# Order of the logarithm and the taps in a state-space mixer, and residual loads ahead of an inverse transform

## The chip, the core and the metric

The kernel runs on one core of one Trainium2 chip. A core has a matrix engine (TensorE, PE in the profile, with its weight loads as PEld), a vector engine (VectorE, DVE), an activation engine (ScalarE, ACT), a general engine (GpSimd, POOL) and SyncE (SP), whose only work here is to issue DMAs. Sixteen DMA engines move data between DRAM and the on-chip memory SBUF; matmuls write to PSUM. Everything is float32. The metric is the device time of one execution in microseconds: before the change 1432.75 us, the median of three runs (1431.81 to 1436.02).

## The reference, cut to what matters

The input is x of 8 images, 1024 tokens each, 128 channels. Three layers follow each other, each added to a residual:

```python
x = x + _L0_conv_ref(_gn(x), ...)               # attention, 4 heads of 32
t = _to_tokens(x)
t = t + _L1_attn_ref(_ln_t(t), ...)             # state-space mixer, both directions
t = t + _L1_ffn_ref(_ln_t(t), ...)              # spectral filters
```

The mixer computes, for each direction, a projection of the normalised tokens into a gate z, a part x, B, C and step sizes dt. x, B and C pass through a causal convolution of four taps and Silu; dt is a softplus:

```python
conv = sum((xp[:, i:i + l, :] * conv_w[:, i] for i in range(K))) + conv_b
xbc = jax.nn.silu(conv)
dt = jax.nn.softplus(dt + dt_bias)
```

The states of 64-token chunks are then built, carried from chunk to chunk with a decay, and read by C; the result is multiplied by silu(z), normalised and projected to 128 channels. The second direction does the same on the tokens in reverse.

The last layer filters the sequence with 16 spectral filters and their alternating-sign versions, by multiplication in the frequency domain, mixes channels with matrices for each filter, and adds a short autoregressive part.

## The kernel before, in words

**Attention.** The first 460 us or so. A loop over 128 steps (8 images, two halves of the queries, 8 blocks of keys) whose order is written out by hand; the step numbers n decide what of the next stages is slipped in. At steps 113 to 123 the first image's tokens are turned and its step sizes computed by the generator `steps` (L482), whose `yield`s cut it into pieces: matmuls for dt (L495), bias and negative absolute value on DVE (L504 to L507), Exp on ACT (L509), 1 + e on DVE and Ln on ACT (L512, L514), and the rest on DVE (L516 to L521).

**Mixer.** About 460 to 1000 us. There are 16 units, one for each image b and direction d (0 forward, 1 backward), in the order (0,0), (0,1), (1,0) and so on. The order on every engine, SP included, is the order of the program text (`manual_schedule(engines=ALL_IN_ORDER)`), so an instruction that waits holds back everything behind it on its engine. In the body of the loop over units, `u` is the unit whose states are built, `following` the one whose inputs are prepared, and `last` the one whose outputs are finished. In a forward unit `fresh` is the next image, whose tokens are turned and whose step sizes are computed piece by piece with `next(going)`. This is so in the units 0, 2, 4, 6, 8, 10 and 12.

The steps that the change and the prediction touch, in their order within a unit: `project_x` and `copy_x` of `following` (L935, L955); `end(last)` with its output projection (`spo`, L1166), sums of squares and reciprocal root; `first_tap(following, 0)` on ACT (L960); `scale_rows(last)` on ACT (L1204); the piece of `steps` with Ln; two of the three other taps of block 0 of `following` on DVE (`convolve`, L968); the two gates of `u`, each a projection on PE (`pz`, L935) and a Silu on ACT (L981); `first_tap(following, 1)`; `from_row` on POOL, a difference of cumulated decays (L912), which carries a written dependency on the last DVE operation of `convolve` so that it runs beside the states; a Relu pair on ACT (L922); `chunk_states` on PE (`pst`, L1070) and `pass_states` on DVE (a copy L1084, then 28 products L1087); the last piece of `steps`; the remaining tap of block 0, its Silu (L973), `project_bc` on PE (`pb`, L990), `activate_bc` on ACT (L1006), and the taps of block 1. PSUM tiles of projections, `pb` and the transposes share one pool of two buffers (`ps_w`), so `pb` waits until the first gate has been read. The states use another pool (`ps_s`).

An activation function belongs to a table set. The compiled program loads a set (`ACT_TABLE_LOAD`) where the next function needs another one than the current: Exp before Ln is one change, Ln before Silu another.

**Filters.** From about 1000 us the tokens are transformed; from 1116 us a loop over 16 chunks of 8 frequencies makes matrices on PE (`matrices`, L1500, from a tile `mst`), copies them to a tile `gs` (two buffers; L1511 and L1513), multiplies the spectra `u` with them (`apply`, L1534), and stores the sums to DRAM (`yd`, L1557). For the first of four output pieces, `fetch` (L1565) brings back each chunk's sums into `early_yt`. In this stage the scheduler keeps the program's order on PE, DVE, ACT and POOL, and places the DMA issues of SP itself.

**Tail.** Four pieces (k, h): two halves of the token blocks by two halves of the images. For each, `yt` (2 MB, two DMAs, L1600) and `res` (1 MB of the residual stream `xa`, L1602) are loaded; DVE forms four sums and differences `z` (L1608); PE makes four products of 128 x 512 over two terms (L1613); DVE multiplies by `keep`, adds the residual in place (L1620), and ACT's queue stores 1 MB (L1623). The pieces' pools are opened after those of the filter stage: two buffers for `yt`, three for `res`, four PSUM buffers.

Of the kernel before, what the change touches and what calls it, by code (L numbers as in the profile page):

```python
# [14 lines left out]
P = 128  # L15
# [30 lines left out]
def fast_kernel(ctx: ExitStack, tc: tile.TileContext, a: dict, out: bass.AP, bad: bass.AP):  # L46
# [433 lines left out]
    def steps(b, seq, pd):  # L480
# [31 lines left out]
        nc.vector.tensor_scalar(u, e, 1.0, None, ALU.add)  # L512
        lg = small("sp_l")
# [77 lines left out]
    with ExitStack() as s:  # L591
# [182 lines left out]
        for n in range(len(units) + 2):  # L774
# [33 lines left out]
            elif n == 113:  # L808
                turn_tokens(0, seqs[0], ps_t.tile([P, T], F32, tag="t", name="px0"))
            elif n == 117:  # L810
                sizes = steps(0, seqs[0], ps_t.tile([P, T], F32, tag="t", name="pd0"))
                for _ in range(3):
                    next(sizes)
            elif n in (121, 123):
                next(sizes, None)
# [10 lines left out]
    with ExitStack() as s:  # L826
# [438 lines left out]
        for at, u in enumerate(units[:-1]):  # L1265
# [46 lines left out]
            convolve(following, 0, range(pad - 1))  # L1312
# [3 lines left out]
            first_tap(following, 1)  # L1316
            for _ in normalized(b, bridge, *norm) if u.d else ():
                pass
# [8 lines left out]
            convolve(following, 0, range(pad - 1, pad))  # L1327
# [86 lines left out]
    with ExitStack() as s:  # L1414
        mp = s.enter_context(tc.tile_pool(name="c_m", bufs=1, side="right"))
        mst = mp.tile([P, 32, C], F32, name="mst")
# [68 lines left out]
        with ExitStack() as s2:  # L1485
# [80 lines left out]

            chunks = NF // FC
            gs, us, gathered = {}, {}, {}
            s2.enter_context(tc.manual_schedule(engines=IN_ORDER))
            for c in range(-1, chunks):  # L1570
                if c + 1 < chunks:
                    gs[c + 1] = p2.tile([P, P, C], F32, tag="gs", name=f"gs{c + 1}")
                    us[c + 1] = loaded_spectra(c + 1)

# [14 lines left out]
        with ExitStack() as s2:  # L1589
            p2 = s2.enter_context(tc.tile_pool(name="i_2", bufs=2))  # L1590
            p3 = s2.enter_context(tc.tile_pool(name="i_3", bufs=3))
            ps_o = s2.enter_context(tc.tile_pool(name="i_ps_o", bufs=4, space=PSUM))

            def loaded(k, h):

                yt = early_yt
                if k or h:
                    yt = p2.tile([P, 2, 4, 4, C], F32, tag="yt", name=f"yt{k}_{h}")
                    for i in range(2):
                        nc.sync.dma_start(yt[:, i], yd[:, k, h * 4 : h * 4 + 4, i])  # L1600
                res = p3.tile([P, 4, 4, C], F32, tag="res", name=f"res{k}_{h}")
                nc.sync.dma_start(res, xa[h * 4 : h * 4 + 4, :, NB - 1 - k].rearrange("b p r c -> p b (r c)"))  # L1602
                return yt, res

            def back(k, h, yt, res):
                z = p2.tile([P, 2, 2, 4, C], F32, tag="z", name=f"z{k}_{h}")
# [3 lines left out]
                for r in (0, 2, 1, 3):  # L1610
                    po = ps_o.tile([P, 4, C], F32, tag="o", name=f"pz{k}_{h}_{r}")
                    for i in range(2):
                        nc.tensor.matmul(  # L1613
                            po,
                            lhsT=inv[:, r, i, :],
                            rhs=z[:, r // 2, i] if r % 2 else yt[:, i, :, r // 2, :],
                            start=(i == 0),
                            stop=(i == 1),
                        )
                    nc.vector.scalar_tensor_tensor(  # L1620
                        res[:, :, r, :], po, keep[:, blk : blk + 1], res[:, :, r, :], ALU.mult, ALU.add
                    )
                nc.scalar.dma_start(  # L1623
                    out[h * 4 : h * 4 + 4, blk * 512 : (blk + 1) * 512].rearrange("b (p r) c -> p b (r c)", r=4), res
                )

            pieces = [(k, h) for k in range(NB) for h in range(2)]
            got = [loaded(*piece) for piece in pieces[:3]]
            for n, piece in enumerate(pieces):
                back(*piece, *got[n])  # L1630
                if n + 3 < len(pieces):
                    got.append(loaded(*pieces[n + 3]))
# [806 lines left out]
```

## Time and profile before

| | us |
|---|---|
| median of three runs | 1432.75 |
| the profiled execution | 1432.01 |
| its span, first to last instruction | 1430.2 |
| PE busy | 1334.7 (93%) |
| DVE busy | 1095.4 (77%) |
| ACT busy | 914.5 (64%) |
| POOL busy | 529.5 (37%) |
| last product of the filter stage ends | 1380.1 |
| last addition of a residual ends | 1423.2 |

Lines of the timeline give the start in us from the span's beginning, the busy time, engine, line of the source, operation, what it writes and reads (`out<-in`), and in brackets the engine's idle time before it with what ended that. Lines of the list of waits give who waited, for whom, the sum in us, how often, and the longest. A line of the table by slices gives the slice, its length, busy time and instructions of PE, PEld, DVE, ACT and POOL, the granted clock of PE (1.00 is full), the mean busy share of the DMA engines, and the GB/s that they moved. SPq and ACTq are DMA issues. A float32 matmul appears as two records.

### The profile page before, as it was taken

To read this page: it belongs to the slowest core of one execution; us is meant where nothing else is said; L and a number is where in the kernel's file an instruction comes from. 1 tells how busy PE (TensorE), PEld (TensorE's weight loads), DVE (VectorE), ACT (ScalarE), POOL (GpSimd) and SP (SyncE) were. 2 spreads that over 40 slices of the span, in tenths; PEclk is the share of its full clock that TensorE was granted. 3 is DMA by queue.
4 is the path that set the end of the run, shared out by engine and by line. 5 is a ranking of instruction groups with operands and counts; after the bars stand their busy time and mean duration, and the time that the engine had idled before them with its cause. 6 is when DMAs were issued, how large, how long until landed. Compare 5 with 4: busy or idle time off the path is not lost. (4 is left out here: it accounts for less than half of the span.)

```text
span 1430.2 us, 45285 instructions
## 1 busy us (share of the span) xinstructions
PE 1334.7 (93%) x19782; PEld 839.8 (59%) x19782; DVE 1095.4 (77%) x2138; ACT 914.5 (64%) x1421; POOL 529.5 (37%) x510
## 2 busy tenths in 40 slices
PE   5999999999998899999999999998799899999977
PEld 2323333233333566666666666666689899999963
DVE  5779888788768588979787988889644677777745
ACT  3665666766757678778787878786454555555520
POOL 3327866875610243324242424233476111111100
PEclk9999999999999899999999999999999999999989
DMA  7100111110000433434343444442459232222258
GB/s 182 40 1 21 55 38 38 38 51 25 8 1 19 102 76 79 100 90 105 75 105 88 94 92 114 95 106 46 132 190 232 73 89 76 71 77 70 72 153 324
DMA packets 139382, 123.09 MB, mean 86 GB/s; under 512 B 44808, under 2 KB 118152, under 8 KB 135080
## 3 DMA queue, kind: packets, MB, share of 16 engines
q1 hardware_dynamic: 137064, 115.93, 31.6%
q8 instruction: 157, 2.57, 0.8%
q10 hardware_dynamic: 2112, 4.19, 0.8%
q14 instruction: 49, 0.40, 0.1%
HBM read 78.15 MB, written 34.08 MB: 78 GB/s over the span
## 5 line engine op out<-in xcount | busy, mean ns | idle before, releaser
L696 ACT ACTIVATE pr<-pt 128x1024 f32<-128x1024 f32 x256 | 248.1, 1021 | 115.1 <-PE pt L691 113.5
L721 DVE TENSOR_TENSOR two<-pr,pr 128x1024 f32<-128x1024 f32 x128 | 162.9, 1313 | 20.5 <-ACT pr L696 19.6
L1513 ACT COPY gs<-pg 128x512 f32<-128x512 f32 x256 | 132.6, 602 | 64.4 <-PE pg L1500 47.9
L1511 DVE COPY gs<-pg 128x512 f32<-128x512 f32 x256 | 158.7, 682 | 15.3 <-PE pg L1500 9.6
L691 PE MATMUL pt<-q,k 32*128 32x512 f32 x1024 | 159.8, 654 | 7.0 <-ACT pr L696 4.7
L1500 PE MATMUL pg<-taps,mst 32*128 32x128 f32 x4096 | 146.0, 281 | 4.9 <-ACT gs L1513 4.1
L1500 PEld LDWEIGHTS pg<-taps,mst 32*128 32x128 f32 x4096 | 134.0, 189 | 17.1 <-issue 11.6
L712 PE MATMUL po<-pr,v 128*32 128x512 f32 x1024 | 139.9, 605 | 0.0
L926 POOL TENSOR_TENSOR ec<-ec,ct 128x2048 f32<-128x2048 f32 x16 | 83.4, 5212 | 135.3 <-ACT cums L868 59.2
L990 PE MATMUL pb<-bxt,wbc 128*128 128x512 f32 x256 | 116.9, 610 | 13.9 <-ACT zs L981 11.3
L1534 PE MATMUL py<-gs,u 128*32 128x128 f32 (+1 forms) x4096 | 127.8, 277 | 0.0
L968 DVE SCALAR_TENSOR_TENSOR xs<-xp,cw,xs 128x1024 f32<-128x1024 f32 x96 | 121.8, 1281 | 3.5 <-issue 1.7
L1534 PEld LDWEIGHTS py<-gs,u 128*32 128x32 f32 (+1 forms) x4096 | 112.0, 140 | 7.2
L1523 POOL TENSOR_SCALAR u<-u 128x512 f32<-128x512 f32 x16 | 24.0, 1498 | 229.3 <-PE pg L1500 128.5
L691 PEld LDWEIGHTS pt<-q,k 32*128 32x128 f32 x1024 | 47.6, 186 | 85.0 <-issue 32.2
L990 PEld LDWEIGHTS pb<-bxt,wbc 128*128 128x128 f32 x256 | 48.2, 193 | 73.1 <-issue 55.6
L1087 DVE SCALAR_TENSOR_TENSOR state<-state,dec,pst 128x64 f32<-128x64 f32 x448 | 87.3, 274 | 1.1
L1196 POOL TENSOR_TENSOR rms<-rms_v,mhalf 128x8 f32<-128x8 f32 x16 | 27.2, 1698 | 161.2 <-DVE rms_v L1194 161.2
L712 PEld LDWEIGHTS po<-pr,v 128*32 128x32 f32 x1024 | 27.8, 109 | 88.5 <-issue 84.6
L912 POOL TENSOR_TENSOR lm<-cs,lm 128x2048 f32<-128x2048 f32 x16 | 57.9, 3621 | 50.2 <-DVE xs L968 33.8
L732 PE MATMUL pd<-two,ones 128*32 128x512 f32 x512 | 73.0, 613 | 0.2
L1166 PEld LDWEIGHTS spo<-wo,y 128*128 128x128 f32 x512 | 62.1, 191 | 15.3 <-issue 10.3
(280 smaller groups left out, 2763.8 us busy)
## 6 DMA issues: line engine op xcount, KB each, us to landing
lm<-cd SPq DMA_DIRECT2D x32, 512.0 KB
ec<-cd SPq DMA_DIRECT2D x32, 512.0 KB
ud<-sp SPq DMA_DIRECT2D x8, 1024.0 KB
u<-ud SPq DMA_DIRECT2D x32, 256.0 KB
yd<-sums SPq DMA_DIRECT2D x32, 256.0 KB
moved<-state SPq DMA_DIRECT2D x48, 128.0 KB
yt<-yd SPq DMA_DIRECT2D x6, 1024.0 KB
X<-in_x SPq DMA_DIRECT2D x8, 512.0 KB
```

The lines of the kernel that those rows point to most:

```text
L691: nc.tensor.matmul(pt[:, i, :], lhsT=k[rows, j * P : (j + 1) * P], rhs=q[rows, cols], start=True, stop=True)
L696: nc.scalar.activation(pr[:, 2 * g : 2 * g + 2, :].rearrange("p i t -> p (i t)"), pt.rearrange("p i t -> p (i t)"), AF.Exp, scale=SCALE,)
L712: nc.tensor.matmul(po[rows, :], lhsT=vs[b][:, j, rows], rhs=pr[:, h, :], start=(j == 0), stop=(j == NT - 1))
L721: nc.vector.tensor_tensor(two, sums["pr"][:, 2 * g : 2 * g + 2, :], pr[:, 2 * g : 2 * g + 2, :], ALU.add)
L926: t = nc.gpsimd.tensor_tensor(u.ec, u.ec, u.ct.unsqueeze(1).to_broadcast([P, NH, NT, L]), ALU.mult)
L968: u.convolved = nc.vector.scalar_tensor_tensor(acc, xp[:, at : at + T], cw[u.d][:, n, i : i + 1], acc, ALU.mult, ALU.add)
L990: nc.tensor.matmul(u.pb[:, i * 512 : (i + 1) * 512], lhsT=wbc[u.d][:, k, :], rhs=xt[:, at : at + 512], start=(k == 0), stop=(k == KC - 1),)
L1087: nc.vector.scalar_tensor_tensor(u.state[:, k, h, :], u.state[:, k - 1, h, :], u.dec[:, c, h, j : j + 1], u.pst[c][:, j, h, :], ALU.mult, ...
L1500: nc.tensor.matmul(pts[g][:, e, :], lhsT=mst[rows, n * 4 + e, :], rhs=taps[rows, cols].rearrange("p f q m i -> p (f q m i)"), start=True, ...
L1511: nc.vector.tensor_copy(to, frm)
L1513: nc.scalar.copy(to, frm)
L1534: nc.tensor.matmul(py[t * 32 : t * 32 + 32 - 16 * m, q // 2, :], lhsT=u[:, i, m:, :, :, q * FC + f].rearrange("p k b i -> p (k b i)"), rhs ...
```

## The change

Three edits stand in the mixer. In `steps`, a further `yield` separates 1 + e on DVE from Ln on ACT; in the loop over units a `next(going, None)` after `first_tap(following, 1)` runs Ln there, behind both gates. In forward units all three taps of block 0 (`soon = pad - u.d`) go ahead of `chunk_states` and `pass_states`; in backward units two, as before. In the attention loop, step 120 runs the piece that step 121 began with.

Three more concern the tail. `res` is no longer a tile per piece: the two blocks' residuals lie in the room of `mst` (block 1, 2 MB) and in a third `gs` tile named `room` (block 0), which also takes the three later `yt`. Three of the four residual loads' bytes (block 1 whole, block 0 for the first four images) are issued in the last pass over the chunks, and the rest between the second and third `yt`. All loads stand ahead of the pieces in the text. The tail uses the filter stage's pools (`u` buffers for `z`, eight PSUM buffers) and its fixed order. The last piece is worked and stored in two halves of two images each, with products of 128 x 256.

```diff
@@ steps
         nc.vector.tensor_scalar(u, e, 1.0, None, ALU.add)
+        yield
         lg = small("sp_l")
         nc.scalar.activation(lg, u, AF.Ln)
@@ attention loop
-            elif n in (121, 123):
+            elif n in (120, 121, 123):
                 next(sizes, None)
@@ loop over units
-            convolve(following, 0, range(pad - 1))
+            soon = pad - u.d
+            convolve(following, 0, range(soon))
             for n in range(2):
                 project_z(u, n)
                 activate_z(u, n)
             first_tap(following, 1)
+            next(going, None)
...
-            convolve(following, 0, range(pad - 1, pad))
+            convolve(following, 0, range(soon, pad))
@@ filter stage
-        mst = mp.tile([P, 32, C], F32, name="mst")
+        mst = mp.tile([P, 32, C], F32, tag="mst", name="mst")
...
+            def load_residuals(k, b, n):
+                nc.sync.dma_start(
+                    res[k][:, b : b + n].rearrange("p b r c -> p b (r c)"),
+                    xa[b : b + n, :, k].rearrange("b p r c -> p b (r c)"),
+                )
...
+                else:
+                    room = p2.tile([P, P, C], F32, tag="gs", name="room")
+                    res = [room[:, :32, :], mp.tile([P, 32, C], F32, tag="mst", name="res1")]
+                    res = [t.rearrange("p (b r) c -> p b r c", b=B) for t in res]
+                    load_residuals(1, 0, B)
+                    load_residuals(0, 0, 4)
@@ tail
+            pieces = [(k, h) for k in range(NB) for h in range(2)]
+            yts = [early_yt]
+            for n, (k, h) in enumerate(pieces[1:], 1):
+                yts.append(room[:, 32 * n : 32 * n + 32].rearrange("p (i b q) c -> p i b q c", i=2, b=4))
+                for i in range(2):
+                    nc.sync.dma_start(yts[n][:, i], yd[:, k, h * 4 : h * 4 + 4, i])
+                if n == 2:
+                    load_residuals(0, 4, 4)
+            for yt, (k, h) in zip(yts, pieces):
+                z = p2.tile([P, 2, 2, 4, C], F32, tag="u", name=f"z{k}_{h}")
...
+                size = 2 if (k, h) == pieces[-1] else 4
+                for b in range(0, 4, size):
+                    bs = slice(b, b + size)
+                    to = res[blk][:, h * 4 + b : h * 4 + b + size]
+                    for r in (0, 2, 1, 3):
+                        po = ps_g.tile([P, 4, C], F32, tag="g", name=f"pz{k}_{h}_{b}_{r}")[:, :size]
...
+                        nc.vector.scalar_tensor_tensor(
+                            to[:, :, r, :], po, keep[:, blk : blk + 1], to[:, :, r, :], ALU.mult, ALU.add
                         )
+                    nc.scalar.dma_start(
...
```

More of the change, by code (lines that the diff above doesn't have):

```diff
@@ L1587, in fast_kernel @@
             fetch(chunks - 1)
[L1589 to L1606, printed above, removed]
+            pieces = [(k, h) for k in range(NB) for h in range(2)]
[8 more added lines that the diff above has]
+                z = p2.tile([P, 2, 2, 4, C], F32, tag="u", name=f"z{k}_{h}")
                 for r, i, op in ((0, 0, ALU.subtract), (0, 1, ALU.add), (1, 0, ALU.add), (1, 1, ALU.subtract)):
@@ L1609, in back @@
                 blk = NB - 1 - k
[L1610 to L1618, printed above, removed]
-                        )
-                    nc.vector.scalar_tensor_tensor(
-                        res[:, :, r, :], po, keep[:, blk : blk + 1], res[:, :, r, :], ALU.mult, ALU.add
-                    )
@@ L1623, in back @@
[L1623 to L1632, printed above, removed]
+                size = 2 if (k, h) == pieces[-1] else 4
@@ new lines, in fast_kernel @@
+                for b in range(0, 4, size):
[3 more added lines that the diff above has]
+                        po = ps_g.tile([P, 4, C], F32, tag="g", name=f"pz{k}_{h}_{b}_{r}")[:, :size]
+                        for i in range(2):
+                            nc.tensor.matmul(
+                                po,
+                                lhsT=inv[:, r, i, :],
+                                rhs=z[:, r // 2, i, bs] if r % 2 else yt[:, i, bs, r // 2, :],
+                                start=(i == 0),
+                                stop=(i == 1),
+                            )
+                        nc.vector.scalar_tensor_tensor(
+                            to[:, :, r, :], po, keep[:, blk : blk + 1], to[:, :, r, :], ALU.mult, ALU.add
+                        )
+                    nc.scalar.dma_start(
+                        out[h * 4 + b : h * 4 + b + size, blk * 512 : (blk + 1) * 512].rearrange(
+                            "b (p r) c -> p b (r c)", r=4
+                        ),
+                        to.rearrange("p b r c -> p b (r c)"),
+                    )
```

## The prediction

> **What bounds the kernel now.** I read the busy shares by stage first, then the list of what TensorE (PE) waited for in the mixer (about 482 to 1000 us of the span), then one unit of the mixer engine by engine, then the last 50 us in order of time and in slices. PE is busy 490.9 of the 518.4 us from 481.6 to 1000, so the mixer goes at PE's pace and only PE's few waits can be won there. The list of PE's waits between 470 and 1040 us starts like this:
>
> ```profile
> PE pb L990 <- ACT zs L981: 11.3, 15, 1.5
> PE sb L1036 <- DVE xdt L1022: 6.6, 15, 0.4
> ```
>
> The first line says that the projection of B and C (`pb`) waited 11.3 us in 15 units for the gates' Silu (L981): `pb` takes the PSUM buffer that the first gate's projection held. In the timeline the seven forward units that also prepare new step sizes wait 0.20 (the first), 1.20 five times and 1.52 us, the backward units 0.46. One such unit on ACT:
>
> ```profile
> 630.00 2.15 ACT L1204 ACTIVATE y<-spo,rms 128x128 f32<-128x128 f32 x8
> 632.17 1.28 ACT L514 ACT_TABLE_LOAD   x1
> 633.46 0.26 ACT L514 ACTIVATE sp_l<-sp_u 128x64 f32<-128x64 f32 x1
> 633.74 1.28 ACT L981 ACT_TABLE_LOAD   x1
> 635.03 1.94 ACT L981 ACTIVATE zs<-pz 128x1024 f32<-128x1024 f32 x2
> ...
> 637.99 2.00 ACT L922 ACTIVATE lm<-lm 128x1024 f32<-128x1024 f32 x2
> 642.94 1.06 ACT L973 ACTIVATE xs<-xs 128x1024 f32<-128x1024 f32 x1 [2.95 <-DVE xs L968]
> ```
>
> The logarithm and its table stand ahead of the gates (632.17 to 633.74, 1.57 us), and ACT later idles 2.95 us for the last tap. PE and DVE in the same unit:
>
> ```profile
> 632.93 1.98 PE L1070 MATMUL pst<-xdd,bg 64*64 64x128 f32 x64
> 636.11 7.14 PE L990 MATMUL pb<-bxt,wbc 128*128 128x512 f32 x16 [1.20 <-ACT zs L981]
> ```
> ```profile
> 630.24 2.60 DVE L968 SCALAR_TENSOR_TENSOR xs<-xp,cw,xs 128x1024 f32<-128x1024 f32 x2
> 634.94 0.29 DVE L1084 COPY state<-pst 128x128 f32<-128x128 f32 x1 [2.11 <-PE pst L1070]
> ```
>
> DVE is idle 2.11 us between its second tap and the first state: room for a third tap of 1.28 us.
>
> The tail begins when PE ends its products at 1380.1. Its timeline:
>
> ```profile
> 1381.84 0.37 SPq L1602 DMA_DIRECT2D res<-xa  x1
> 1383.65 0.64 SPq L1565 DMA_DIRECT2D early_yt<-yd  x2
> ...
> 1389.59 6.59 PE L1613 MATMUL pz<-early_yt,inv 128*128 128x512 f32 x8 [9.50 <-DMA res<-xa]
> ...
> 1416.65 1.98 PE L1613 MATMUL pz<-yt,inv 128*128 128x512 f32 x4 [1.57 <-DMA yt<-yd]
> ...
> 1420.52 2.73 DVE L1620 SCALAR_TENSOR_TENSOR res<-pz,keep,res 128x512 f32<-128x512 f32 x4 [1.30 <-DMA res<-xa]
> ```
> ```profile
> 1387.00:1388.00 1.00, 0.00 (x0) 0.00 (x0) 0.00 (x0) 0.00 (x0) 0.00 (x0) 0.50 1.16 90
> 1390.00:1391.00 1.00, 1.00 (x2) 0.40 (x2) 0.42 (x1) 0.00 (x0) 0.00 (x0) 0.50 1.04 387
> ```
>
> A residual load of 1 MB was issued ahead of the last fetch of early_yt. Its bytes fill 1383 to 1387; the fetch then crawls (90 GB/s, DMA full) to about 1389, and PE starts at half clock (the 0.50). From 1390 to 1420 DMA is full at 385 to 410 GB/s: 6 MB of yt, 4 of residuals, 4 of output. The last piece waits for its yt and for its residual, which waited for an earlier store to free its buffer.
>
> **What the Trainium skill says.** "ScalarE: Activation LUTs", section "What ACT_TABLE_LOAD costs", gives 1283 ns and 1380 ns of drain for a switch. This trace has 1.28 us, and no drain (load at 632.17, next activation at 633.46); I use 1.29. "DMA: Bandwidth & Descriptors", section "Queues, rings and completion order": a queue's descriptors are taken in ring order, and two queues alternate by packet. That agrees with the fetch standing behind the residual. "TensorE: Matmul & The Clock Gate", section "What's actually happening": the clock halves after an idle window of about 3.4 us that runs free, and returns after a busy one. Here it halved about 5 us after PE stopped and came back about 6 us after PE began.
>
> **The mixer, part by part.** PE's order is unchanged. On ACT the Ln moves behind both gates and the first tap of block 1; the changed order shows Silu's load before the gates, Ln's load before Ln, and one new Silu load before L973: 7 x 1.29 = 9.0 us more ACT work. In the unit above: Silu load 632.17, first gate done about 634.5, before `pst` ends at 634.91. So the whole wait goes in each of the seven units: 0.20 + 5 x 1.20 + 1.52 = **7.7 us**. What must follow in time:
> - Third tap on DVE: 632.84 to 634.1, states still at 634.94. The seven waits there are 1.05 (unit 0), 2.11 or 1.79. Unit 14 has only 0.29, so its states come 1.0 us later; its second half needs them moved by 981.6 and has them at about 981.2. Cost 0.
> - POOL's lm (L912, 3.62 us) waits for the third tap: 634.2 to 637.9 instead of 636.6. Behind it on ACT stands the Relu pair. ACT reaches it at 638.1 anyway (gates to 635.4, tap 1.13, load and Ln 1.57).
> - The new Silu load then runs 640.0 to 641.3, L973 starts at 641.3 instead of 642.94, since its taps are long done; bt and ct follow at 642.4, 0.3 us behind the new end of `pb` (642.05). DVE's block-1 taps come 1.28 earlier. The transposes of the next unit start at 647.9 and their x is ready at about 646.8. Without the old 2.95 us idle the load would cost up to 1.29 per unit.
>
> In the attention loop, u is computed one step earlier and Ln stays at its step: 0.
>
> **The tail.** On SP the load of 2 MB now stands ahead of the third-last store of sums and goes when the last matrices are made (mst free about 1371.2); the one of 1 MB stands ahead of the second-last and goes at 1374.8. At 389 GB/s they run about 1372.4 to 1381.2, under the last 9 us of products, which read nothing from DRAM. The stores of sums and a fetch queue behind their bytes; only the last store (issued 1381.41) decides, and its bytes can start at about 1382.2 instead of 1382.0. The two issues take SP 0.4 to 0.6 us each while it otherwise waits for DVE.
> - Start: the last fetch still goes at 1383.65, now with nothing ahead. From about 1384.9 it needs the same 2.2 us; PE starts at about 1387.6 instead of 1389.59: 2.0.
> - Clock: PE is idle 7.5 us instead of 9.5, so it still drops. Before, 5.9 cold us cost 2.95; I take 2.6.
> - PE work is 16 records of 0.43 us a piece, 6.87; four pieces 27.5. The split last piece has twice the records at half the columns; no row shows 128x256 of this form, bounds 0 (0.21 each) to +3 (no gain from fewer columns), I take 0. Loads behind the start: yt 1392.4, yt 1397.8, last residual 1402, last yt about 1411.5, sharing with two stores. Piece 3 could begin at 1387.6 + 2.6 + 20.6 = 1410.8; its yt and its four z (2.5 us) cost about 1.0. PE ends at 1418.7; before 1421.9.
> - The last product's addition ends 0.6 us later, 1419.3, against 1423.25.
> - The last store is 0.5 MB. Before, 6.95 us lay between the last addition and the end, of which 3.0 were its bytes; half the bytes leave 5.45. End at 1424.7 against 1430.2: **5.5 us**.
>
> Sum 13.2: a span of 1417.0, a run of 1418.8 by the profiled execution's 1432.01, and 1419.5 by the median of 1432.75, 0.74 above it.
>
> **Rivals.** (a) Mixer gain only. For it: 3 MB more on a full queue at the end of the products, where PE's own instruction packets travel too, and the fetch could be pushed by several us. Each us by which the 3 MB run past 1381 moves the start as much; 5.5 us would undo the tail. Against: from 1372 to 1380 the DMA engines moved only 69 to 107 GB/s. 1432.75 - 7.7 = 1425. (b) Tail gain only: PE finds another wait within 1.2 us in each unit, say x for the transposes (slack 0.93 before). 1432.75 - 5.5 = 1427.3. Against it: every successor of `pb` above moves by 1.2 or more. (c) Slower: the chain tap, POOL's lm, Relu, new load, L973, bt, ct, second x. If DVE's idle before the states (2.11) and ACT's before L973 (2.95) were not real room, it grows by 1.28 + 1.29 in seven units, 18 us; less 5.5, about 1445. It decides once the chain's delay passes 2.95 + 0.93 = 3.9 us; I count 2.6. (d) Clock windows fall luckily, PE stays fast in the tail: 1416.5, inside my own range.
>
> **How the numbers follow.** Likeliest (both gains, with d) 0.72, own range 1414.5 to 1423.5; (a) 0.12; (b) 0.10; (c) 0.03; a mixture near no change 0.03. A shift of 10 us also moves the clock windows at other stage starts, some 2 us either way. About 0.3% (4.3 us) is what a measurement here can tell from no change. The range 1414.5 to 1426.5 leaves out part of (b), (c) and the edges. Faster 0.92, same 0.05, slower 0.03.
>
> **What would show it.** Right: PE's wait of `pb` for L981 falls from 11.3 to about 3.6 us, forward units last 1.2 us less, three loads of tables a forward unit, L973 no longer waiting for L968; PE starting its tail about 7.5 us after its last product, and 5.5 us from the last addition to the end. Wrong: a new wait on ACT before `bt`, `sx` or `sy`, a gap in the products after 1371, or a tail start later than 9.5 us after the products.

## The result and the profile after

The changed kernel takes 1422.1 us in the median (1421.0 to 1425.1), the kernel before 1434.2 us beside it (1431.8 to 1436.0): a ratio of 0.992, interval 0.9897 to 0.9943. The profiled execution took 1422.16 us with a span of 1420.2, against 1432.01 and 1430.2. The forecast was 1419.5 us with a range from 1414.5 to 1426.5.

**The mixer.** The list of PE's waits between 470 and 1040 us, changed kernel:

```profile
PE pb L991 <- ACT zs L982: 3.6, 8, 0.5
```

It answers to the 11.3 us in 15 units shown of before. Eight units are left with 0.45 us each: the backward ones, which prepare no step sizes. The seven forward units don't wait there any more. The same forward unit as before on ACT, in the timeline:

```profile
630.03 1.28 ACT L982 ACT_TABLE_LOAD   x1
631.32 1.94 ACT L982 ACTIVATE zs<-pz 128x1024 f32<-128x1024 f32 x2
633.15 1.24 ACT L961 ACTIVATE xs<-xp,cb,cw 128x1024 f32<-128x1024 f32 x1
634.40 1.28 ACT L515 ACT_TABLE_LOAD   x1
635.70 0.26 ACT L515 ACTIVATE sp_l<-sp_u 128x64 f32<-128x64 f32 x1
635.86 1.99 ACT L923 ACTIVATE lm<-lm 128x1024 f32<-128x1024 f32 x2
637.85 1.28 ACT L974 ACT_TABLE_LOAD   x1
639.15 1.06 ACT L974 ACTIVATE xs<-xs 128x1024 f32<-128x1024 f32 x1
```

The gates come first, the logarithm (L515) after them, and there are three loads of tables where there were two. ACT is never idle in these lines: the new load of 1.28 us stands where ACT idled 2.95 us for the last tap. PE and DVE in that unit:

```profile
630.79 1.98 PE L1071 MATMUL pst<-xdd,bg 64*64 64x128 f32 x64
632.70 7.14 PE L991 MATMUL pb<-bxt,wbc 128*128 128x512 f32 x16
```
```profile
628.09 3.92 DVE L969 SCALAR_TENSOR_TENSOR xs<-xp,cw,xs 128x1024 f32<-128x1024 f32 x3
632.80 0.29 DVE L1085 COPY state<-pst 128x128 f32<-128x128 f32 x1 [0.80 <-PE pst L1071]
```

`pb` follows the states at once, without the bracket of 1.20 us that it had. DVE does three taps in one row, and of its 2.11 us ahead of the states 0.80 is left.

**The tail.** The timeline of the changed kernel from the last products on (rows of PE, DVE and SP's queue):

```profile
1358.89 4.83 PE L1537 MATMUL py<-gs,u 128*32 128x128 f32 x164
1358.99 0.39 SPq L1571 DMA_DIRECT2D res<-xa  x1
...
1362.66 0.42 SPq L1571 DMA_DIRECT2D room<-xa  x1
...
1365.36 3.76 PE L1537 MATMUL py<-gs,u 128*32 128x128 f32 x128 [1.63 <-issue]
...
1371.57 1.12 PE L1537 MATMUL py<-gs,u 128*32 128x128 f32 x28 [2.45 <-issue]
...
1380.20 5.19 PE L1628 MATMUL pz<-early_yt,inv 128*128 128x512 f32 x8 [7.50 <-DMA early_yt<-yd]
...
1405.77 1.61 PE L1628 MATMUL pz<-room,inv 128*128 128x256 f32 x6 [2.79 <-DMA room<-yd]
...
1414.24 0.48 DVE L1635 SCALAR_TENSOR_TENSOR room<-pz,keep,room 128x256 f32<-128x256 f32 x1 [0.38 <-PE pz L1628]
```

Before, the 320 last products were one row of 9.00 us:

```profile
1371.09 9.00 PE L1534 MATMUL py<-gs,u 128*32 128x128 f32 x320
```

Now they stop twice, 1.63 and 2.45 us, and "issue" says that PE waited for nothing that the profile shows. The first residual load is issued as these products begin. From the products' end to the tail's first one it is 7.50 us instead of 9.50. The last spectra arrive 2.8 us late, and the last addition ends 5.5 us ahead of the end.

### The profile page after: what moved, and what is told of

Its sections match the earlier page's. It is cut to its first block, busy times and chain, and to the rows that moved or that the text cites. A ratio compares the mean times of both kernels' runs of the same rounds, so it can differ in the third digit from the quotient of the medians.

```text
span 1420.2 us, 45312 instructions
## 1 busy us (share of the span) xinstructions
PE 1331.6 (94%) x19798; PEld 840.4 (59%) x19798; DVE 1096.5 (77%) x2142; ACT 923.1 (65%) x1428; POOL 528.5 (37%) x510
## 5 line engine op out<-in xcount | busy, mean ns | idle before, releaser
L1503 PEld LDWEIGHTS pg<-taps,mst 32*128 32x128 f32 x4096 | 133.0, 188 | 16.6 <-issue 11.5
L1537 PEld LDWEIGHTS py<-gs,u 128*32 128x32 f32 (+1 forms) x4096 | 112.4, 140 | 11.9 <-issue 4.6
```

Of the source, the lines that this page charges most:

```text
L1503: nc.tensor.matmul(pts[g][:, e, :], lhsT=mst[rows, n * 4 + e, :], rhs=taps[rows, cols].rearrange("p f q m i -> p (f q m i)"), start=True, ...
L1537: nc.tensor.matmul(py[t * 32 : t * 32 + 32 - 16 * m, q // 2, :], lhsT=u[:, i, m:, :, :, q * FC + f].rearrange("p k b i -> p (k b i)"), rhs ...
```

## The same stretches in all kernels

The tables are used by the experiments that follow. The first gives the medians, each kernel against runs of the kernel before taken beside it; us of gain are (1 - ratio) x 1432.75.

| kernel | median, us | ratio to before, interval | gain, us |
|---|---|---|---|
| mixer and attention edits alone | 1423.5 | 0.9941 (0.9921 to 0.9961) | 8.5 |
| tail edits alone | 1430.0 | 0.9983 (0.9974 to 0.9993) | 2.4 |
| logarithm alone | 1426.3 | 0.9958 (0.9938 to 0.9977) | 6.0 |
| third tap alone | 1433.0 | 0.9991 (0.9979 to 1.0004) | 1.3 |
| mixer edits and idle loads | 1426.4 | 0.9967 (0.9954 to 0.998) | 4.7 |
| changed, three quarters of the residual set to zero | 1419.4 | 0.9899 (0.9873 to 0.9924) | 14.5 |
| changed, loads placed later in the text | 1422.1 | 0.9917 (0.9883 to 0.995) | 11.9 |
| changed, loads behind the products | 1423.9 | 0.9949 (0.9932 to 0.9966) | 7.3 |
| changed, loads late and stores on SP | 1423.2 | 0.9936 (0.9913 to 0.9959) | 9.2 |
| changed, SP in order | 1430.9 | 0.9977 (0.9961 to 0.9994) | 3.3 |
| the same, stores on SP | 1424.2 | 0.9938 (0.9918 to 0.9957) | 8.9 |
| changed, transfers of the end rearranged | 1417.9 | 0.9903 (0.9886 to 0.9921) | 13.9 |

The second is worked out from PE's timeline of one profiled execution of each kernel: from the end of the last group of matrices to the end of the products, from there to the tail's first product, from that to the end of the tail's last product, and to the end of the span, in us.

| kernel | products (gaps in them) | to the tail | tail products (waits in them) | to the end | sum |
|---|---|---|---|---|---|
| before | 8.9 (0) | 9.5 | 32.5 (1.6) | 8.1 | 59.0 |
| changed | 13.7 (4.1) | 7.5 | 34.0 (2.8) | 6.0 | 61.2 |
| mixer and attention edits alone | 8.9 (0) | 9.3 | 33.3 (3.4) | 9.1 | 60.7 |
| tail edits alone | 14.2 (2.9) | 7.4 | 31.2 (1.5) | 6.4 | 59.2 |
| mixer edits and idle loads | 12.0 (2.3) | 7.2 | 36.2 (4.8) | 8.5 | 63.9 |
| three quarters zero | 11.0 (1.6) | 6.7 | 29.8 (0) | 7.1 | 54.5 |
| loads placed later in the text | 12.6 (2.3) | 7.6 | 30.4 (0) | 7.0 | 57.5 |
| loads behind the products | 8.9 (0) | 15.6 | 29.8 (0) | 6.5 | 60.8 |
| loads late, stores on SP | 8.9 (0) | 15.8 | 30.2 (0) | 6.5 | 61.4 |
| SP in order | 10.4 (0.5) | 6.9 | 39.3 (5.0) | 6.1 | 62.7 |
| SP in order, stores on SP | 9.9 (0) | 6.7 | 33.0 (2.2) | 8.4 | 58.0 |
| transfers rearranged | 8.9 (0) | 8.5 | 30.0 (0) | 9.0 | 56.4 |

## Experiments

My theory on seeing the two traces side by side: the mixer gave what was forecast, and the tail lost part of its gain to its own early loads, because PE's instructions come by DMA too and stood behind them. The rivals: the gain of the mixer comes from elsewhere; the gaps come from the new tail's code or from the clock.

**The two halves of the change.** The first kernel has the mixer and attention edits with the tail of before, the second the tail edits alone on the kernel before. Their diffs are the halves of the diff shown above.

> The mixer's and attention's edits alone, the tail as before. The theory of the prediction: seven waits of pb for the gates go, 7.7 us, so about 1426 us against 1434 before, and PE's wait of pb for the gates near 3.6 us. A rival, that most of the 12 us measured for the whole change is luck of the clock's windows and the mixer gave less, expects under 4 us. A rival that the whole change's gain is the tail's expects no difference.

> The tail's edits alone, mixer and attention as before. The prediction's tail: 5.5 us faster than before, about 1428.5. The theory of the starved instructions (the early residual loads hold up PE's instruction packets, some 4.8 us of gaps in the last products): 1 to 3 us slower than before, about 1436, with the same two gaps of about 1.6 and 2.5 us without a releaser in the last products.

Measured: ratios of 0.9941 and 0.9983. The mixer's edits give 8.5 us (5.6 to 11.3), the tail's 2.4 us (1.0 to 3.7). Both forecasts for the tail missed: it is neither 5.5 us faster nor, as the theory of the starved instructions had it, slower, though gaps of 2.65 and 0.23 us are there. The last products of the first kernel, and PE's waits of the second from 1354 us on:

```profile
1360.27 9.01 PE L1537 MATMUL py<-gs,u 128*32 128x128 f32 x320
```
```profile
PE py L1534 <- issue: 2.9, 2, 2.6
PE pz L1625 <- DMA room<-yd: 1.5, 1, 1.5
```

With the old tail the 320 products run through; with the new one they stop, whatever the mixer does. The two gains add up to 10.9 us, near the 11.5 of both together (0.8% of 1432.75). So the 7.7 us of the mixer stand, and the 5.5 us of the tail don't: they lie outside its interval. In the profiled executions the stretch from the last matrices on is no shorter with the tail edits (59.2 against 59.0 us), although the median gains 2.4. That execution was 2.4 us ahead at its last matrices already, where the program text is the same. Single profiles differ by so much; for the size of the tail's gain the medians count, for its parts the stretches. Where in the tail the 2.4 us of the medians arise is therefore not shown.

**Logarithm and tap apart.** On the kernel before, first the logarithm, then the tap:

```diff
         nc.vector.tensor_scalar(u, e, 1.0, None, ALU.add)
+        yield
         lg = small("sp_l")
...
-            elif n in (121, 123):
+            elif n in (120, 121, 123):
...
             first_tap(following, 1)
+            next(going, None)
```
```diff
-            convolve(following, 0, range(pad - 1))
+            soon = pad - u.d
+            convolve(following, 0, range(soon))
...
-            convolve(following, 0, range(pad - 1, pad))
+            convolve(following, 0, range(soon, pad))
```

> The kernel before with the later logarithm alone (the pause ahead of it and the two places where the generator is moved on); taps and tail stay as before. Theory (the wait of the wide products for the gates is the whole gain of the mixer): PE's wait for the gates in the mixer of the first direction falls from 11.3 to about 3.6 us, and the time from about 1432.7 to about 1425.0 us, as far as the kernel with both mixer edits went (1423.5, ratio 0.994). Rival (the third tap carries part of it, since VectorE's convolution sits ahead of the gates' additions): the wait falls less, to 6 us or more, and the time only to 1428 or so.

> The kernel before with the third tap on VectorE ahead of the states as its only edit; logarithm and tail as before. Theory (the tap fills an idle place of VectorE and frees ScalarE's wait for the last tap, which PE meets only once the logarithm has left the gates): the wait of the wide products for the gates stays at about 11.3 us, PE doesn't wait for the second x, ScalarE's idle time ahead of the second x (20.6 us in the kernel before) goes, and the time is that of the kernel before, ratio 0.998 to 1.002. Rival (the tap gives its part by itself): the time falls by the 2 to 3 us by which the kernel with both mixer edits stood below the one with the logarithm alone, ratio 0.998 or less.

PE's waits from 470 to 1040 us with the logarithm alone:

```profile
PE pb L991 <- ACT zs L982: 3.6, 8, 0.5
...
PE sx L1020 <- ACT xs L974: 2.8, 6, 0.6
```

and what ACT waited for ahead of the second operation on x (the view of the tile `xs`), again with the logarithm alone:

```profile
L974 ACT ACTIVATE xs<-xs x28: 1044/1057/1060, 509.7 to 947.0; 128x1024 f32<-128x1024 f32 x28
its engine sat idle before it (us, times) until:
  DVE xs L969: 11.9, 7
```

The logarithm alone takes the same 7.7 us off the wait of `pb` as both edits do. But 2.8 us come back at the transposes (`sx`) of six units: the new load of a table and the logarithm now stand in ACT's path to x, and ACT still idles 11.9 us for the tap that comes late. With the tap alone that idle time is gone from ACT's list, yet nothing is gained that can be measured:

```profile
PE pb L990 <- ACT zs L981: 11.1, 14, 1.5
```

So neither the theory nor the rival of the first expectation was quite right; the theory of the second holds. The wait fell in full, and the time fell by 6.0 us, near the 4.9 of 7.7 less 2.8. With both mixer edits the list has no line of `sx` waiting for `xs`. By the waits, then, the tap is worth nothing by itself and 2.8 us beside the logarithm. The medians (8.5 less 6.0) agree, but their intervals overlap. The interval of the tap's own run, 0.9979 to 1.0004, reaches a little past the 0.998 that the rival named, so a small gain by itself isn't excluded.

**Loads that nobody reads.** The kernel with the mixer edits and the old tail, plus the two early loads into free buffers:

```diff
+                else:
+                    room = p2.tile([P, P, C], F32, tag="gs", name="room")
+                    spare = [room[:, :32, :], mp.tile([P, 32, C], F32, tag="mst", name="spare1")]
+                    spare = [t.rearrange("p (b r) c -> p b r c", b=B) for t in spare]
+                    for k, n in ((1, B), (0, 4)):
+                        nc.sync.dma_start(
+                            spare[k][:, :n].rearrange("p b r c -> p b (r c)"),
+                            xa[:n, :, k].rearrange("b p r c -> p b (r c)"),
+                        )
```

> The kernel with the mixer and attention edits and the tail of before, plus the same two loads of 2 and 1 MB beside the last products, into buffers that nothing reads: the load alone, without any use of it. Theory (the loads delay PE's instruction packets): idle time of 3 to 4.5 us put down to issue appears in the last products, where the same kernel without the loads has none, 15 to 16 us from the last matrices to the products' end, and the time goes from about 1423.5 to about 1427 us. Rival (the gaps belong to the new tail's code, its buffers and order, not to traffic): no gap, 11.2 us, and 1423 to 1424 us.

PE's last products in its timeline:

```profile
1360.46 8.33 PE L1537 MATMUL py<-gs,u 128*32 128x128 f32 x292
1371.12 1.36 PE L1537 MATMUL py<-gs,u 128*32 128x128 f32 x28 [2.32 <-issue]
```

The loads alone make the gap, 2.3 us here, and the gain over the kernel before falls from 8.5 to 4.7 us (the intervals just overlap). The gap is smaller than I expected, and its sign and place are right; from the start of the last group of matrices to the products' end it is 14.2 us, short of the 15 to 16. The stops lie at fixed places of the instruction stream: after 164 and 292 of the 320 products in the changed kernel and with the tail edits alone, after 292 here. 128 products with their weight loads are 256 instructions. The view of the DMA queues counts the packets; first the kernel with the mixer edits alone from 1360 to 1370 us, then the changed one from 1358 to 1373 us (columns: packets, MB, share of the 16 engines):

```profile
q1 hardware_dynamic: 368, 0.66, 19.0%
q8 instruction: 3, 0.05, 1.9%
```
```profile
q1 hardware_dynamic: 1896, 3.74, 70.8%
q8 instruction: 2, 0.03, 0.8%
```

Three packets of instructions of some 16 KB in 10 us, with little beside them; two in 15 us beside 3.74 MB. The traces' records of the packets give their times. With the mixer edits alone a packet starts every 3.3 to 3.9 us. In the changed kernel 6.5 and 6.0 us lie between them (1356.54, 1362.99, 1368.97); the late ones have landed at 1363.95 and 1370.00, and PE goes on at 1365.36 and 1371.57, 1.4 and 1.6 us later. In the other kernels too each stop put down to issue in the last products ends 1.4 to 1.6 us after the landing of a packet that started 5.0 to 7.2 us behind the one before. So the experiment shows that the loads cause the gaps, and the packets' times show by which way.

**Fewer or later loads.** In the first kernel the three early quarters of the residual are set to zero by POOL instead of loaded, so that they are missing in the output. In the second I moved the loads behind the products in the program text.

```diff
-                    load_residuals(1, 0, B)
-                    load_residuals(0, 0, 4)
+                    nc.gpsimd.memset(res[1], 0.0)
+                    nc.gpsimd.memset(res[0][:, 0:4], 0.0)
```
```diff
-                    load_residuals(1, 0, B)
-                    load_residuals(0, 0, 4)
...
             yts = [early_yt]
+            load_residuals(1, 0, 4)
...
-                if n == 2:
-                    load_residuals(0, 4, 4)
+                load_residuals(*((1, 4, 4), (0, 0, 4), (0, 4, 4))[n - 1])
```

> The whole change, but the three early quarters of the residual are filled with zeros by POOL at the same place instead of being loaded, so these residuals are left out of the output. Starved instructions: the same tiles are written at the same time, no DMA runs, so the two gaps in the last products go and the kernel is about 4.8 us faster than the whole change, about 1417. Rival, that the gaps come from waits for the reused tiles or from writes to SBUF beside PE's reads: the gaps stay, about 1422.

> The whole change, but no residual is loaded before the products end: each quarter is loaded in front of or behind a later yt, as before the change in order. Starved instructions: no gaps in the last products (4.8 us less), but 3 MB more in the tail, 8.1 us at 389 GB/s where DMA bounds it: about 1424 to 1426. The prediction's view (early loads free of cost, tail bound by PE): 4 to 6 us slower than the whole change, 1426 to 1428, with no difference in the last products.

The second did not do what it was meant to. SP's order is left to the scheduler in this stage, and it put the loads beside the products again:

```profile
1362.37 0.93 SPq L1571 DMA_DIRECT2D res<-xa  x2
```

A gap of 2.3 us stayed, and the run says nothing on loads that come after the products. In the first kernel the one remaining load was moved up as well, to 1363.5 us, and one gap of 1.6 us came with it, again with a late packet (6.5 us): 1 MB seems to be enough, though POOL was filling the tiles from 1361.5 to 1366.9 us. Without the other 3 MB nothing waited in the tail, and the stretch from the last matrices took 54.5 us instead of 61.2. In these two executions the 3 MB cost 6.7 us in all, beside the products and later. By the ratios it is 3.0 us, with intervals that overlap; the median, 1419.4 us, lies between the 1417 of the theory and the 1422 of the rival.

**Loads kept back for certain.** ACT's order is fixed by the text, so the loads go on its queue: in the first kernel behind the last gather, in the second (second diff, in place of the loop after the chunks) behind the third of the last four gathers, and there the stores go on SP's queue:

```diff
             def load_residuals(k, b, n):
-                nc.sync.dma_start(
+                nc.scalar.dma_start(
...
-                    load_residuals(1, 0, B)
-                    load_residuals(0, 0, 4)
...
+            for part in ((1, 0, B), (0, 0, 4), (0, 4, 4)):
+                load_residuals(*part)
             fetch(chunks - 1)
...
-                if n == 2:
-                    load_residuals(0, 4, 4)
```
```diff
                         gather(c, half, turn, py)
+                        if c + 1 == chunks and n == 2:
+                            for part in ((1, 0, B), (0, 0, 4), (0, 4, 4)):
+                                load_residuals(*part)
...
-                    nc.scalar.dma_start(
+                    nc.sync.dma_start(
                         out[h * 4 + b : h * 4 + b + size, blk * 512 : (blk + 1) * 512].rearrange(
```

> The changed kernel with its three residual loads issued by ScalarE's queue after the copy of the last gather, so that no load runs beside the last products; ScalarE's order is fixed by the code, so they can't be moved ahead. Theory (PE runs dry because its instruction packets queue behind the loads' packets): no idle time put down to issue in the last products, and 11.2 us from the last group of matrices to the products' end, where the changed kernel took 16.0. The loads then meet the fetch of the first spectra and the loads of the others: the wait ahead of the tail grows from 7.5 to 9 to 12 us and the wait of 2.8 us inside it to 3 to 6, so the end is at 1418 to 1423 us. Rival (the gaps come from the products themselves, the code's new order or the clock, and not from the loads): gaps of 3 to 4 us remain in the products, and the end is later than that of the changed kernel, 1424 or more.

> The changed kernel with two edits: the three residual loads are issued by ScalarE's queue after the third of the four last gathers, when PE's packets for the last products should have been fetched, and the stores of the output by SP's queue, behind the loads of the spectra. Theory (packets late behind loads; loads of spectra late behind stores): at most 1 us of idle time put down to issue in the last products, about 11.5 us from the last matrices to the products' end, and the wait of 2.8 us for the last spectra gone; 1422.1 less 4.1 less 2.8 is 1415 us, 1414 to 1418 with the fetch of the first spectra somewhat later beside the loads. Rival (the gaps come from elsewhere, and the loads of the spectra are bound by the total of bytes, not by their order): 1421 to 1424 us, gap and wait as in the changed kernel.

The gaps are gone in both, the products take 8.9 us, and nothing waits inside the tail. So far the theory. But both end later than forecast, the second within the range of its rival though gap and wait are gone, since the tail begins 15.6 and 15.8 us after the products instead of 7.5. The chain that ended last, in the kernel with the loads behind the products:

```profile
1370.41 6.63 DMA yd<-sums
1377.04 7.69 issue
1384.72 29.77 PE pz L1626 x80
```

and PE's longest wait in the other kernel, from 1354 us on:

```profile
PE pz L1627 <- DMA early_yt<-yd: 15.8, 1, 15.8
```

The last store of sums takes 6.63 us, and the next 7.69, which the chain puts down to nothing, go to the fetch behind it, as the second line names it; both are slow beside 4 MB of residual. I had allowed 9 to 12 us for this and a wait of 3 to 6 us later. Here loads ahead of the fetch cost about as much as loads beside the products (60.8 and 61.4 us against 61.2): they stand in front of something else.

**SP in order.** The whole filter stage and tail with SP's order fixed: fetch, then in turn 1 MB of residual and the next spectra. The second kernel adds the second diff, the stores on SP's queue.

```diff
-            s2.enter_context(tc.manual_schedule(engines=IN_ORDER))
+            s2.enter_context(tc.manual_schedule(engines=ALL_IN_ORDER))
...
-                    load_residuals(1, 0, B)
-                    load_residuals(0, 0, 4)
...
                         gather(c, half, turn, py)
-                if c > 0:
-                    fetch(c - 1)
+                    if c > 0 and n == 1:
+                        fetch(c - 1)
             fetch(chunks - 1)
+            load_residuals(1, 0, 4)
...
-                if n == 2:
-                    load_residuals(0, 4, 4)
+                load_residuals(*((1, 4, 4), (0, 0, 4), (0, 4, 4))[n - 1])
```
```diff
-                    nc.scalar.dma_start(
+                    nc.sync.dma_start(
                         out[h * 4 + b : h * 4 + b + size, blk * 512 : (blk + 1) * 512].rearrange(
```

> The changed kernel with SP's order fixed in the filter stage and the tail: the fetch of the last spectra first, then in turn 1 MB of residual and the 1 MB of the next spectra, in the order of their use, and nothing of the residual beside the last products or ahead of the fetch. The fetch of the chunk before is issued in the middle of the last one. Theory (the changed kernel lost what its loads took from PE's instruction packets, and the kernels with held loads lost it again by loads ahead of the fetch): no idle time put down to issue in the last products, 11.2 us from the last matrices to the products' end, at most 8 us from there to the tail's first product, no wait for the last spectra. 1422.1 less 4.1 to 4.8 less 2.8 is 1414.5 to 1415.2 us; 1413 to 1418. Rival (the tail is bound by the bytes it still has to move, 11 MB): the products of the tail wait 3 us or more for the loads that no longer run early, and the end is at 1420 us or later.

> The same as the kernel with SP's order fixed, and the stores of the output on SP's queue too, behind all loads. Theory (a store on ScalarE's queue shares the engines with the loads still on their way, but here the loads are all ahead of PE's need): no more than 1 us from the kernel without it. Rival (stores beside loads delay the last spectra): the wait for the last spectra is there in the kernel without this edit and gone here, 2 to 3 us apart.

PE's waits from 1350 us on, first without and then with the stores on SP:

```profile
PE pz L1626 <- DMA early_yt<-yd: 6.9, 1, 6.9
PE pz L1626 <- DMA room<-yd: 5.0, 2, 3.0
PE py L1537 <- issue: 0.5, 1, 0.5
```
```profile
PE pz L1626 <- DMA early_yt<-yd: 6.7, 1, 6.7
PE pz L1626 <- DMA room<-yd: 2.2, 2, 1.4
```

The start is as expected, 6.9 and 6.7 us after the products. The spectra are late all the same, by 5.0 us with the stores on ACT's queue and by 2.2 with them on SP's. So the rival of the first expectation came true: PE waits more than 3 us for loads that no longer run early, and the end is later than 1420 us. The difference of 2.8 us is what the rival of the second expectation named (stores beside loads delay the last spectra), but the wait isn't gone, and each kernel has one profile: the first one's took 1436.3 us, the longest of its 14 runs. The ends, 1430.9 and 1424.2 us, are no better than that of the changed kernel. Some of the first was lost in the filter stage, where PE was busy 77.7 of the 80 us from 1120 to 1200, and 80.0 both in the second and in the changed kernel. Why it lost time there I didn't find out; the second kernel has the same code in that stage. Nor are the last products as quick as the 8.9 us elsewhere: they take 10.4 and 9.9 us, in the first with a gap of 0.5 us without any residual beside it, behind a packet that came after 5.0 us.

**The transfers of the end rearranged.** SP in order from the last chunk on only. 1 MB of residual goes on ACT's queue some 3 us ahead of the products' end, the rest in turn with the spectra, the first two stores behind all loads on SP's queue, the other three on ACT's.

```diff
-            def load_residuals(k, b, n):
-                nc.sync.dma_start(
+            def load_residuals(k, b, n, queue=nc.sync):
+                queue.dma_start(
...
-                    load_residuals(1, 0, B)
-                    load_residuals(0, 0, 4)
+                    s2.enter_context(tc.manual_schedule(engines=ALL_IN_ORDER))
...
                         gather(c, half, turn, py)
-                if c > 0:
+                    if c == chunks - 1 and n == 1:
+                        load_residuals(1, 0, 4, nc.scalar)
+                        fetch(c - 1)
+                if 0 < c < chunks - 1:
                     fetch(c - 1)
...
-                if n == 2:
-                    load_residuals(0, 4, 4)
+                load_residuals(*((1, 4, 4), (0, 0, 4), (0, 4, 4))[n - 1])
...
-                    nc.scalar.dma_start(
+                    (nc.scalar if k else nc.sync).dma_start(
                         out[h * 4 + b : h * 4 + b + size, blk * 512 : (blk + 1) * 512].rearrange(
```

> The changed kernel with its transfers of the end in another order. SP's order is fixed from the last chunk on only (the filter stage keeps the scheduler's). The first 1 MB of residual is issued by ScalarE's queue after the second of the four last gathers, some 3 us ahead of the products' end, when PE's last packets should be in; the fetch of the last spectra follows alone, then in turn the next spectra and 1 MB of residual; the first two stores go on SP's queue behind all loads, the last three on ScalarE's. Theory (the tail loses by what runs beside the packets, beside the fetch and ahead of the spectra): no gap in the last products, 9 us from the last matrices to their end, 7 from there to the tail's first product, 30 to 31 to its last one without a wait of 1 us or more, 6 to the end: 52 to 53 us from the last matrices to the end, where the changed kernel took 61.2 and the one with the old tail 60.7. The time is then about 1415 us, 1413 to 1418. Rival (the end is bound by its bytes, or the packets still come late with 1 MB beside them): 58 us or more in that stretch and 1420 us or later.

Its timeline:

```profile
1360.00 9.01 PE L1537 MATMUL py<-gs,u 128*32 128x128 f32 x320
...
1365.70 0.39 ACTq L1571 DMA_DIRECT2D res<-xa  x1
...
1377.49 5.41 PE L1629 MATMUL pz<-early_yt,inv 128*128 128x512 f32 x8 [8.48 <-issue]
...
1400.90 7.51 ACTq L1639 DMA_DIRECT2D out<-room  x3
...
1407.51 0.48 DVE L1636 SCALAR_TENSOR_TENSOR room<-pz,keep,room 128x256 f32<-128x256 f32 x1 [0.38 <-PE pz L1629]
```

No gap with 1 MB beside the last 3 us of the products, no wait inside the tail, 1417.9 us. By the ratios this is 2.4 us better than the changed kernel (0.9903 against 0.992, but the intervals overlap), and 5.4 us better than the mixer edits with the old tail (0.9941; the two intervals meet at 0.9921). The stretch is 56.4 us, not the 52 to 53 of the theory: the start came 8.5 us after the products instead of 7, and from the last addition to the end it is 8.5 us (1407.99 to 1416.5) where the changed kernel had 5.5: the stores that had stood back come last, and DMA still moves 374 to 392 GB/s until 1412 us. The time is in the range of the theory and the stretch between the two forecasts: the order of the transfers counts, as the theory says, and the end waits for bytes, as the rival says.

## Why the prediction was right or wrong

- **The mixer, right in its sum and its mechanism.** The wait of `pb` for the gates fell from 11.3 to 3.6 us, the 7.7 forecast; the runs give 8.5 (5.6 to 11.3). The extra load of a table was hidden in ACT's idle time, as said, and so was the third tap in DVE's 2.11 us, of which 0.80 is left. The prediction had counted both as costs of nothing. The 1380 ns of drain that the Trainium skill adds to each load ("ScalarE: Activation LUTs", "What ACT_TABLE_LOAD costs") are absent here too: the load at 634.40 is followed by the activation at 635.70. The runs add what the tap is for: without it 2.8 of the 7.7 us are lost at the transposes, which is what the prediction's "without the old 2.95 us idle the load would cost up to 1.29 per unit" came to: some 0.47 in each of six units.
- **The tail, wrong in its first step.** "Under the last 9 us of products, which read nothing from DRAM" is the step that failed. PE's instructions come by DMA at that very time, in packets that started 6.5 and 6.0 us apart beside the loads instead of 3.3 to 3.9. The products took 13.7 us instead of 8.9, +4.8, where the sum had 0. Rival (a) named PE's packets on the full queue as its reason, and the list of signs named "a gap in the products"; both were given too little weight. The runs showed the cause by adding the loads alone and by taking them away. One reading of the tail was too large as well: the 14 MB (6, 4 and 4) that the prediction puts between 1390 and 1420 us are those of the whole tail; 11.9 MB moved in that window.
- **The start, right.** 7.5 us after the products, as forecast, instead of 9.5.
- **Spectra and clock mis-sized, split piece right.** The last spectra were given 1.0 us and took 2.8 out of PE's time. After that idle time the clock was down once more: the slices show 0.58, 0.50 and 0.50 from 1407 to 1410 us, and eight records took 3.40 us (1407.18 to 1410.58) where the next eight took 1.73. The forecast had nothing for this 1.7. The cold stretch at the tail's start was given 2.6 and cost 1.6: eight records took 5.02 us (1380.20 to 1385.22), the next eight 3.44. The split piece cost nothing, as taken: eight records of 256 columns go in 1.73 us (1410.58 to 1412.31), 0.22 each, half of 0.43. So the tail's products took 34.0 us where the forecast had 31.1.
- **The end, right.** 5.5 us from the last addition to the end, 5.45 forecast.

In the profile these terms make the stretch 2.2 us longer (4.8 - 2.0 + 1.5 - 2.1) where 5.5 less was forecast; by the medians the tail edits gain 2.4. The whole, 1422.1 us, is 2.6 above the forecast; by the medians the tail fell short by 3.1.

That the whole came so near is in part luck. In the profiles the changed kernel begins its last group of matrices 12.2 us ahead (1356.72 against 1368.92), where the sum had 7.7. From the first product of the states to the last it gained 7.8 us (497.1 to 985.7 against 498.8 to 995.2). The other 4.4 lie before and behind, where the edits take no wait away, and there the granted clock was higher: 0.93 against 0.86 from 450 to 500 us, and 0.96 (1000 to 1120) against 0.93 (1010 to 1130) where the filter stage begins. The kernel with the tail edits alone, whose mixer is the old one, has 0.93 from 450 to 500 too, so this is the chance of the clock that the prediction put at some 2 us.

## What to carry to other kernels

A stretch without loads of its own isn't free room for transfers: the instructions of a busy engine come the same way, and a long row of small instructions runs dry (320 products in 9 us) where the tail's 80 products, spread over 30 us or more, ran at full DMA without such a stop. Before a transfer is moved earlier, list everything that will stand behind it, the packets of instructions and the small transfers on the critical path too. Where a serial piece is moved off a wait, look for the next operation that it now delays, and move that operation's other input early in the same edit: the tap takes away no wait of PE alone, and 2.8 us of waits beside the logarithm.

## What was not expected of the hardware

PE stopped for 1.63 and 2.45 us beside a load of 3 MB in the changed kernel, once for 2.3 us beside as much in two others, once for 1.6 us beside 1 MB, and not at all beside 1 MB issued 3.3 us ahead of the products' end.

A stop much shorter than the idle window of about 3.4 us that the prediction quotes can halve the clock. With the tail edits alone it stood at 0.50 behind a stop of 2.65 us, and 128 products took 5.43 us where the changed kernel, at full clock after 1.63 us, took 3.76. Two stops of 2.3 us (idle loads; loads placed later in the text) had the same effect, one of 2.44 us later in the kernel with idle loads had not. The clock's records of all 14 traces fit one reading: its changes lie on a grid of 3.41 us, and what counts is how much of a stop falls into one cell. From 1340 us on, the clock stayed full behind each of 243 cells in which PE stood still for at most 1.92 us, and fell behind each of 32 with 2.01 us or more; of the 2.44 us 1.85 lay in one cell. Earlier in the kernel, with other work, it also fell behind cells with less idle time, so the limit holds for this stretch alone.

And a small transfer suffers much from a large one: the last store of sums, 256 KB, took 2.4 us with the queues quiet (1373.77 to 1376.15 in the kernel with idle loads), 3.7 us while the last of 1 MB of residual was still moving (transfers rearranged) and 6.6 us beside 4 MB.
